# Layer 0: from TensorE transposes to a blocked second load, VectorE block transposes and a norm on ScalarE

## The chip, the cores and the metric

The kernel runs on one core of one Trainium2 chip. The time is device microseconds for one execution of the whole kernel (both layers). In the profile PE is TensorE (PEld its weight loads), DVE is VectorE, ACT is ScalarE, POOL is GpSimd, and SP is the engine whose queue issues nearly all DMAs.

## What is computed

`x` is 1 x 128 x 256 x 256 in float32. Two layers each add an attention branch to it. The first one, which the change touches, is this, cut to what matters here:

```python
def _gn(v, G=32, eps=1e-5):                 # mean and variance of 32 groups of 8 channels
    ...
    return ((g - m) / jnp.sqrt(s + eps)).reshape(v.shape)

def _L0_conv_ref(m, z, ...):                # m = _gn(x): 128 rows s, 256 positions i, 256 channels
    m_norm = layer_norm(m, ln_m_w, ln_m_b)  # over the channels
    q, k, v = m_norm @ Wq.T, m_norm @ Wk.T, m_norm @ Wv.T      # 8 heads of 32
    b = (z_norm @ Wb.T) ...                 # a bias for each head, the same for all rows s
    gate = jax.nn.sigmoid(m @ Wg.T + bg)
    scores = einsum('bsihc,bsjhc->bshij', q, k) * scale + b
    o = einsum('bshij,bsjhc->bsihc', softmax(scores), v)
    return (o * gate) @ Wo.T + bo

x = x + _L0_conv_ref(_gn(x), ...)
x = x + _L1_conv_ref(_gn(x), ...)           # banded attention, 4 heads of 64
```

## The kernel before, in words

**Stages.** A first stage (about 240 us) reads all of x for the group statistics and turns z into `eb`, the exponential of the bias. Layer 0 then works through 64 *pairs* of rows in about 1,830 us; layer 1 does its own 64 pairs in about 1,260 us. The change lies in layer 0, with a few operations added to the end of the first stage (`norm`).

**A pair.** A `Pair` loads two rows of x into `xt`, 128 partitions by 4 tiles of 256 channels, with positions on the partitions. `centre` and `scale` (POOL, L1233 and L1236) make `xg`, the group-normalised rows. `moments` (DVE) takes each position's mean and variance of `xg`; `root` (POOL) makes the inverse deviation `rs`. `send` stores it to DRAM and `fetch` reads it back spread over all partitions as `rs_r`. `turn` (L1274, L1278) is what the change replaces: TensorE transposes `xg` in eight 128x128 blocks into PSUM and ACT copies the result to `xgT`, channels on the partitions. `normal` (POOL, L1283) multiplies by `rs_r`, in two halves k = 0 and 1 of the channels, giving `xnT`. `project` (L1296, result moved from PSUM by ACT, L1300) makes qT and kT from `xnT` and the gate `gT` from `xgT`; `values` makes v from `xnT`. The layer norm's mean is folded into the weights.

**Attention.** `scores(r, c)` multiplies for row r and channel half c into two PSUM tiles (L1330), and ACT takes the exponential in place (L1337). `add_bias` multiplies by `eb` on DVE into two tiles `e` (L1346) and POOL adds the two key halves into `eboth` (L1351). `apply` makes the weighted values (`ps_ov`) and the sums (`ps_su`). `gate`, `invert` and `normalize` finish the division: `invert` takes the reciprocal, stores it to DRAM as `rsum`, and SP reads it back as four broadcasts `rvb`. `out_row` projects into PSUM and `keep_row` adds the residual.

**Order.** The order on every engine is the program's own (`manual_schedule`). One turn of the loop, 28.77 us long, interleaves five pairs: `old` and `was` are finishing, `now` is in its attention, `nxt` is being transposed and projected, `nn` is being normalised. In PE's order a turn is: scores(0,0), apply of `was`, projections qT and kT with m = 1, values(0), scores(0,1), the two gate projections, `old.out_row(1)`, scores(1,0), apply(0), `nxt.turn()`, values(1), scores(1,1), `nxt`'s projections qT and kT with m = 0, `was.out_row(0)`. All projections, values and output rows share a PSUM ring of two banks (`mm`, two buffers), so each of them needs the result of two steps earlier to have been moved out. The scores (and `ps_x` of `turn`) share the other ring, `ps_s`, of two buffers.

Of the kernel before, what the change touches and what calls it, by code (L numbers as in the profile page):

```python
# [9 lines left out]
F32 = mybir.dt.float32  # L10
AF = mybir.ActivationFunctionType
ALU = mybir.AluOpType
# [4 lines left out]
P = 128  # L17
# [4 lines left out]
def bcast(ap, axis, n):  # L22

    ap = ap.unsqueeze(axis)
    shape = list(ap.shape)
    shape[axis] = n
    return ap.broadcast_to(shape)
# [746 lines left out]
def fast_kernel(  # L774
# [25 lines left out]
    nc = tc.nc  # L800
    S, I, C = x.shape
    CZ = z.shape[2]
    H = wbT.shape[1]
    D0 = C // H
# [3 lines left out]
    NB = I // P  # L808
    KC = C // P
    NP = S // 2  # L810
    N2 = 2 * I
# [4 lines left out]
    const = ctx.enter_context(tc.tile_pool(name="const", bufs=1))  # L816
    dram = ctx.enter_context(tc.tile_pool(name="dram", bufs=1, space=DRAM))

    ident = const.tile([P, P], F32, name="ident")
# [111 lines left out]
    for a in range(KC):  # L931
        for h in range(H1):
            n = P // H1
# [5 lines left out]
    for h in range(H1):  # L939
        n = P // H1  # L940
# [57 lines left out]
    def mm(name):  # L998
        return ps_mm.tile([P, 512], F32, name=name, tag="mm")
# [199 lines left out]
    HQ = P // D0  # L1199
    NT = 2 * NB  # L1200
# [11 lines left out]
    for n in range(RC):  # L1212
# [2 lines left out]
            bcast(ident.rearrange("p (q d) -> p q d", q=HQ)[:, :, n * D0 // RC], 2, D0),  # L1215
        )

    class Pair:


# [7 lines left out]
            )  # L1228


        def centre(self):
            self.xg = la.tile([P, NT, C], F32, name="xg", tag="xg", bufs=2)
            nc.gpsimd.tensor_tensor(self.xg, self.xt, bcast(M0, 1, NT), ALU.subtract)  # L1233

        def scale(self):
# [226 lines left out]
    def some(n):  # L1462
        for _ in range(min(n, len(later))):
            later.pop(0)()
# [10 lines left out]
    def pair(p):  # L1475
        return Pair(p) if p < NP else Nobody()
# [20 lines left out]
    def norm():  # L1497
        nonlocal M0, R0, nxt
        M0, R0 = next(steps)
        now.centre()  # L1500
        now.scale()
        nxt = pair(1)

    def weigh():
# [5 lines left out]

    plan = {
        (0, 4): begin, (1, 1): lambda: next(steps), (1, 3): lambda: next(steps), (1, 4): take, (2, 3): norm,
        (3, 4): weigh,
        (5, 3): lambda: now.send(nc.scalar),
# [13 lines left out]
    behind, nx, n = None, 0, 0  # L1528
# [39 lines left out]
    su = ps_o.tile([P, I], F32, name="ps_su")  # L1568

    with tc.manual_schedule():  # L1570
        old = was = Nobody()
        es = nn3 = None
        for p in range(NP):

            nxt.root()
            nxt.send()
            e0 = now.add_bias(0, 0, now.scores(0, 0))
            was.apply(1, es)
            was.gate(1)
            was.invert()  # L1580
            nxt.fetch()
            nn.centre()
            if p == 0:
                nxt.residual()
            now.project("qT", 1)
            now.project("kT", 1)
            some(1 if p < NP - 2 else 3)
            now.values(0)
            now.keep_values(0)

            es = e0, now.add_bias(0, 1, now.scores(0, 1))
            nn.scale()
            if p == 0:
                now.residual()
            for m in range(KC):
                now.project("gT", m)
            old.out_row(1)
            some(1 if p < NP - 2 else 3)
            old.keep_row(1)

            nn3 = pair(p + 3)
            e0 = now.add_bias(1, 0, now.scores(1, 0))
            now.apply(0, es)
            now.gate(0)
            nxt.turn()
            nxt.normal()
            was.normalize(0)
            now.values(1)
            now.keep_values(1)
            nn.moments(0)  # L1610
            if p == NP - 1:
                some(8)

            es = e0, now.add_bias(1, 1, now.scores(1, 1))
            was.normalize(1)
            nn.residual()
            nxt.project("qT", 0)
            nxt.project("kT", 0)
            nn.moments(1)
            some(3 if p < NP - 2 else 9)  # L1620
            was.out_row(0)
            was.keep_row(0)
            old, was, now, nxt, nn = was, now, nxt, nn, nn3
        was.apply(1, es)
        was.gate(1)
        was.invert()
        old.out_row(1)
        was.spread()
        old.keep_row(1)
        for r in range(2):  # L1630
            was.normalize_last(r)
        for r in range(2):
            was.out_row(r)
            was.keep_row(r)
        some(len(later))
# [28 lines left out]
    with tc.tile_pool(name="l1", bufs=2) as sb, tc.tile_pool(  # L1664
        name="l1s", bufs=4
    ) as sm, tc.tile_pool(name="ps1_mm", bufs=2, space=PSUM) as ps_mm, tc.tile_pool(
        name="ps1_s", bufs=1, space=PSUM
    ) as ps_s, tc.tile_pool(name="ps1_o", bufs=1, space=PSUM) as ps_o:

        def mm1(name):  # L1670
            return ps_mm.tile([P, 512], F32, name=name, tag="mm")
# [173 lines left out]
        def pair1(p):  # L1845
            return Pair1(p) if p < NP else Nobody()
# [15 lines left out]
        with tc.manual_schedule():  # L1862
            now, nxt = pair1(0), pair1(1)
# [18 lines left out]
        with tc.manual_schedule():  # L1882
            was = Nobody()
            for p in range(NP - 1):
                nn = pair1(p + 2)
# [23 lines left out]
                was, now, nxt = now, nxt, nn  # L1909
# [19 lines left out]
        ps = mm1("ok_ps")  # L1929
# [4 lines left out]
@with_exitstack  # L1934
def mixer_kernel(ctx, tc, *args):

    nc = tc.nc
    keep = ctx.enter_context(tc.tile_pool(name="verdict", bufs=1))
    verdict = keep.tile([1, 1], mybir.dt.int32, name="verdict")
    fast_kernel(tc, *args, verdict)  # L1940
    again = nc.values_load(verdict[0:1, 0:1], min_val=0, max_val=1)
    with tc.If(again > 0):
        general_kernel(tc, *args)
# [53 lines left out]
```

## Time and profile before

| | |
|---|---|
| median of 3 runs | 3363.17 us (3362.63 to 3363.67) |
| span of the profiled execution, first to last instruction | 3356.3 us |
| so around the span | about 6.9 us |
| one turn of the layer 0 loop | 28.77 us |
| PE, busy share of the span | 96% |
| the 512 transposes of `turn` | 69.9 us busy, 273 ns each, overlapping |
| the 128 copies to `xgT` on ACT | 68.7 us busy, 589 ns each |
| POOL in a turn | 0.80 busy |
| DVE, ACT in a turn | 0.65 and 0.45 busy |
| DMA engines in a turn | about 0.23 busy |

The profile is one execution of the program. Busy times of different engines lie beside one another; PE's overlap even among themselves, since matmuls are pipelined. The row for the transposes is therefore not what they take out of PE's time; that is read from the starts of the groups in the timeline, or from the chain that ended last.

### The profile page before, as it was taken

How to read it: one execution, taken by the hardware profiler on the slowest of the kernel's cores; microseconds unless marked ns; L12 is line 12 of the kernel's file. 1: busy time of each engine (PE TensorE's matmuls, PEld its weight loads, DVE VectorE, ACT ScalarE, POOL GpSimd, SP SyncE). 2: the span in 40 equal slices, each digit the busy share in tenths (PEclk: the TensorE clock that was granted, in tenths of full speed). 3: DMA queues.
4: the chain of work that ended last, by engine and by line, in shares of the span. 5: the costliest groups of instructions: out<-in, count | busy, mean ns of one | idle time of the engine just before them, and what ended most of it. 6: DMA issues, size and time to landing. Idle time of an engine off the chain costs nothing.

```text
span 3356.3 us, 81416 instructions
## 1 busy us (share of the span) xinstructions
PE 3210.8 (96%) x35168; PEld 2039.6 (61%) x35168; DVE 2021.7 (60%) x3115; ACT 1461.1 (44%) x2121; POOL 1961.9 (58%) x1375
## 2 busy tenths in 40 slices
PE   5389999999999999999999998999999999999998
PEld 3255555555555555555555555667777677677676
DVE  7955666666666666666666666466544444443456
ACT  2264444444444444444444443344444444444443
POOL 2378787777777787887777774333333333333332
PEclk8699999999999999999999999999999999999999
DMA  9941212221222222122212221111211211112111
GB/s 350 369 135 43 74 49 74 74 74 49 74 74 57 58 71 68 49 74 74 74 49 74 74 65 47 64 53 53 65 53 53 65 53 58 60 53 61 57 58 53
DMA packets 198640, 262.39 MB, mean 78 GB/s; under 512 B 46240, under 2 KB 147488, under 8 KB 197120
## 3 DMA queue, kind: packets, MB, share of 16 engines
q1 hardware_dynamic: 193200, 254.19, 24.7%
q8 instruction: 279, 4.57, 0.6%
q10 hardware_dynamic: 5072, 2.90, 0.3%
q14 instruction: 89, 0.73, 0.1%
HBM read 188.30 MB, written 68.75 MB: 77 GB/s over the span
## 4 chain that ended last, share of the span: by engine, by line
PE 91%; DVE 4%; DMA 3%; ACT 1%; POOL 1%; issue 1%; SPq 0%; ACTq 0%; POOLq 0%; DVEq 0%
PE ps_p L1296 20%; PE ps_p L1743 14%; PE ps_sc L1330 8%; PE ps_y L1831 7%; PE ps_ov L1362 7%; PE ps_v L1758 7%; PE ps_y L1417 6%; PE ps_v L1311 6%; PE ps_o L1800 3%; PE ps_sc L1772 3%; PE ps_su L1370 3%; PE ps_x L1274 2%; PE ps_x L1730 2%; PE ps_su L1800 1%; DVE st L1178 1%; DVE zst L1103 1%
## 5 line engine op out<-in xcount | busy, mean ns | idle before, releaser
L1351 POOL TENSOR_TENSOR eboth<-e 128x512 f32<-128x512 f32 x512 | 639.9, 1271 | 391.7 <-DVE e L1346 389.7
L1346 DVE TENSOR_TENSOR e<-ps_sc,eb 128x1024 f32<-128x1024 f32 x512 | 603.2, 1220 | 304.9 <-ACT ps_sc L1337 304.8
L1337 ACT ACTIVATE ps_sc<-ps_sc 128x1024 f32<-128x1024 f32 x512 | 492.8, 1006 | 509.2 <-PE ps_sc L1330 509.2
L1782 POOL TENSOR_TENSOR e<-e,bw 128x384 f32<-128x384 f32 x256 | 258.7, 1031 | 444.3 <-ACT e L1780 444.3
L1743 PE MATMUL ps_p<-xgT,w_in 128*128 128x512 f32 x1024 | 469.2, 601 | 3.7 <-DVE w_in L1701 3.7
L1735 POOL TENSOR_TENSOR xt<-xt,bout_r 128x1024 f32<-128x1024 f32 x64 | 152.0, 2374 | 379.0 <-PE ps_x L1730 379.0
L1835 DVE TENSOR_TENSOR yo<-ps_y,xt 128x512 f32<-128x512 f32 x128 | 88.3, 690 | 379.1 <-PE ps_y L1831 379.1
L1743 PEld LDWEIGHTS ps_p<-xgT,w_in 128*128 128x128 f32 x1024 | 188.9, 190 | 203.0 <-issue 170.9
L1330 PE MATMUL ps_sc<-qT,kT 32*128 32x256 f32 x4096 | 293.3, 400 | 2.0 <-ACT kT L1300 2.0
L1296 PE MATMUL ps_p<-xnT,wq 128*128 128x512 f32 x512 | 266.0, 631 | 3.5 <-POOL xnT L1283 2.9
L1831 PE MATMUL ps_y<-w_out,oT 128*128 128x256 f32 x1024 | 249.1, 386 | 2.6 <-DVE oT L1816 2.6
L1362 PE MATMUL ps_ov<-e,v 128*32 128x256 f32 x4096 | 247.7, 382 | 0.0
L1417 PEld LDWEIGHTS ps_y<-wo,oT 128*128 128x128 f32 x1024 | 194.3, 190 | 82.4 <-issue 59.3
L1417 PE MATMUL ps_y<-wo,oT 128*128 128x256 f32 x1024 | 242.0, 379 | 2.0 <-POOL oT L1407 1.2
L1330 PEld LDWEIGHTS ps_sc<-qT,kT 32*128 32x128 f32 x4096 | 184.9, 184 | 94.4 <-issue 83.6
L1311 PE MATMUL ps_v<-wv,xnT 128*128 128x256 f32 x1024 | 242.2, 379 | 0.0
L1296 PE MATMUL ps_p<-xnT,wk 128*128 128x512 f32 x512 | 240.6, 592 | 0.0
L1296 PE MATMUL ps_p<-xgT,wg 128*128 128x512 f32 x512 | 236.8, 605 | 0.0
L1758 PE MATMUL ps_v<-w_in,xgT 128*128 128x256 f32 x1024 | 231.8, 379 | 0.0
L1813 DVE RECIPROCAL rv<-odd 128x256 f32<-128x256 f32 x128 | 224.4, 1753 | 4.4
L1758 PEld LDWEIGHTS ps_v<-w_in,xgT 128*128 128x128 f32 x1024 | 194.4, 190 | 53.5 <-issue 30.1
L1311 PEld LDWEIGHTS ps_v<-wv,xnT 128*128 128x128 f32 x1024 | 189.6, 190 | 50.8 <-issue 31.0
(170 smaller groups left out, 4958.8 us busy)
## 6 DMA issues: line engine op xcount, KB each, us to landing
xa<-in_x_dram SPq DMA_DIRECT2D x8, 4096.0 KB
xt<-in_x_dram SPq DMA_DIRECT2D x64, 512.0 KB
x<-xo SPq DMA_DIRECT2D x16, 2048.0 KB
xt<-x SPq DMA_DIRECT2D x64, 512.0 KB
rvb<-rsum SPq DMA_DIRECT2D x252, 128.0 KB
out_dram<-yo SPq DMA_DIRECT2D x63, 512.0 KB
zt<-in_z_dram SPq DMA_DIRECT2D x15, 2048.0 KB
rs_r<-rs_d SPq DMA_DIRECT2D x63, 256.0 KB
```

The costliest lines, as they stand in the source:

```text
L1296: nc.tensor.matmul(ps, w[:, k, m * P : (m + 1) * P], getattr(self, src)[:, k, :], start=(k == 0), stop=(k == KC - 1),)
L1311: nc.tensor.matmul(self.ps_v[:, b * C : (b + 1) * C], self.xnT[:, k, t * P : (t + 1) * P], wv[:, k, :], start=(k == 0), stop=(k == KC - 1),)
L1330: nc.tensor.matmul(self.pss[q // 2][:, q % 2, b, :], self.kT[rs, c, r * I + b * P : r * I + (b + 1) * P], self.qT[rs, c, r * I : (r + 1) * I],
L1337: nc.scalar.activation(self.pss[a], self.pss[a], AF.Exp)
L1346: nc.vector.tensor_tensor(e, pss[a], eb[:, h : h + 2], ALU.mult)
L1351: nc.gpsimd.tensor_tensor(t, es[a][:, :, 0, :], es[a][:, :, 1, :], ALU.add)
L1362: nc.tensor.matmul(ov[q * D0 : (q + 1) * D0, c, :], self.v[:, r, b, h * D0 : (h + 1) * D0], es[q // 2][:, q % 2, b, :], start=(b == 0), st ...
L1417: nc.tensor.matmul(self.ps_y[:, b * C : (b + 1) * C], self.oT[r][:, k, b * P : (b + 1) * P], wo[:, k, :], start=(k == 0), stop=(k == KC - 1),)
L1743: nc.tensor.matmul(ps, w_in[:, k, n * C + m * P : n * C + (m + 1) * P], self.xgT[:, k, :], start=(k == 0), stop=(k == KC - 1),)
L1758: nc.tensor.matmul(ps[:, b * C : (b + 1) * C], self.xgT[:, k, t * P : (t + 1) * P], w_in[:, k, 2 * C : 3 * C], start=(k == 0), stop=(k == ...
L1782: nc.gpsimd.tensor_tensor(e[:, q], e[:, q], bcast(bw.rearrange("p b w -> p (b w)"), 1, KC), ALU.mult)
L1831: nc.tensor.matmul(ps[:, b * C : (b + 1) * C], self.oT[r][:, k, b * P : (b + 1) * P], w_out[:, k, :], start=(k == 0), stop=(k == KC - 1),)
```

## The change

For all pairs but the first, `turn` leaves the loop. `blocks` loads the pair's two rows a second time into `xs`, by four DMAs on SP's queue, one for each j of 4. Partition j*32+b then holds, for each n, channel half k and row block, the run of 32 channels `(k, j)` of the position that belongs to b: runs of 128 bytes, 1,024 in each DMA. `turn_blocks` transposes the 32x32 blocks on DVE, two instructions of 128x512, into `xgT`. This is raw x, so `scale_blocks` normalises it on ACT, in place, with two activations that take scale and bias from a column per channel half (`col`). The columns are made once, in `norm`, by four small matmuls and two DVE operations. In the loop `nxt.turn_blocks()` and `nn.blocks()` stand after `now.keep_values(0)`, and `nxt.scale_blocks()` after `nn.scale()`, ahead of the gate projections. `xg` goes from two buffers to one. POOL's `centre` and `scale` stay, because the moments still need `xg`.

```diff
+    col = const.tile([P, 2, KC], F32, name="col")
...
+        def blocks(self):
+
+            self.xs = la.tile([P, NB, KC, 2 * HQ, D0], F32, name="xs", tag="xs", bufs=1)
+            by_block = x[2 * self.p : 2 * self.p + 2].rearrange(
+                "s (i b n) (k j a) -> j b (n k) (s i) a", i=HQ, n=NB, k=KC, a=D0
+            )
+            for j in range(HQ):
+                nc.sync.dma_start(self.xs[j * D0 : (j + 1) * D0].rearrange("b n k i a -> b (n k) i a"), by_block[j])
+
+        def turn_blocks(self):
+            self.xgT = la.tile([P, KC, N2], F32, name="xgT", tag="xgT", bufs=2)
+            for n in range(NB):
+                nc.vector.transpose(
+                    self.xgT.rearrange("p k (s n i b) -> p n k s i b", s=2, n=NB, i=HQ)[:, n],
+                    self.xs[:, n].rearrange("p k (s i) a -> p k s i a", s=2),
+                )
+
+        def scale_blocks(self):
+            for k in range(KC):
+                nc.scalar.activation(
+                    self.xgT[:, k, :], self.xgT[:, k, :], AF.Identity,
+                    bias=col[:, 1, k : k + 1], scale=col[:, 0, k : k + 1],
+                )
+
         def centre(self):
-            self.xg = la.tile([P, NT, C], F32, name="xg", tag="xg", bufs=2)
+            self.xg = la.tile([P, NT, C], F32, name="xg", tag="xg", bufs=1)
...
         M0, R0 = next(steps)
+        ps = mm("ps_col")
+        for n, row in enumerate((R0, M0)):
+            for k in range(KC):
+                nc.tensor.matmul(
+                    ps[:, n * KC + k : n * KC + k + 1], row[:, k * P : (k + 1) * P], ident[:, 0:1],
+                    start=True, stop=True,
+                )
+        nc.vector.tensor_copy(col[:, 0], ps[:, 0:KC])
+        nc.vector.scalar_tensor_tensor(col[:, 1], ps[:, KC : 2 * KC], -1.0, col[:, 0], ALU.mult, ALU.mult)
         now.centre()
...
     with tc.manual_schedule():
+        nxt.blocks()
         old = was = Nobody()
...
             now.values(0)
             now.keep_values(0)
+            nxt.turn_blocks()
+            nn.blocks()
 
             es = e0, now.add_bias(0, 1, now.scores(0, 1))
             nn.scale()
+            nxt.scale_blocks()
             if p == 0:
                 now.residual()
             for m in range(KC):
...
             now.gate(0)
-            nxt.turn()
             nxt.normal()
```

## The prediction

> **What bounds the kernel now.** I read the page's busy shares first, then the chain that ended last, then one turn of layer 0 on each engine. The page and the chain:
>
> ```profile
> PE 3210.8 (96%) x35168; PEld 2039.6 (61%) x35168; DVE 2021.7 (60%) x3115; ACT 1461.1 (44%) x2121; POOL 1961.9 (58%) x1375
> PE 91%; DVE 4%; DMA 3%; ACT 1%; POOL 1%; issue 1%; SPq 0%; ACTq 0%; POOLq 0%; DVEq 0%
> ```
>
> So PE sets the time on average, and work taken from PE looks like time gained. Whether it is depends on what is late next at that place. Pieces of the chain in one turn, start and length:
>
> ```profile
> 999.89 1.86 PE ps_ov L1362 x32
> 1001.76 0.86 PE ps_su L1370 x16
> 1002.62 1.02 PE ps_x L1274 x8
> 1003.64 1.73 PE ps_v L1311 x8
> 1005.37 1.08 PE ps_sc L1330 x16
> 1006.45 3.81 PE ps_p L1296 x8
> ...
> 1015.79 3.63 PE ps_p L1296 x8
> ```
>
> The eight transposes take 1.02 us of PE. The next ps_x starts at 1031.39, so a turn is 28.77 us. The same projection takes 3.63 us elsewhere and 3.81 here: PE already waits 0.18 us inside it. The timelines of PEld and POOL say for what:
>
> ```profile
> 1007.42 0.30 PEld L1296 LDWEIGHTS ps_p<-xnT,wq 128*128 128x128 f32 x2 [0.74 <-POOL xnT L1283]
> ...
> 1002.41 2.51 POOL L1351 TENSOR_TENSOR eboth<-e 128x512 f32<-128x512 f32 x2 [1.63 <-DVE e L1346]
> 1004.86 2.50 POOL L1283 TENSOR_TENSOR xnT<-xgT,rs_r 128x512 f32<-128x512 f32 x2
> ```
>
> The second half of xnT ends at 1007.36, PE continues at 1007.42. Before xnT, POOL does eboth of scores(1,0), having idled 1.63 us for e. This chain hangs on scores(1,0) ending on PE (999.89): exp, e, two eboth, two xnT, 7.5 us. It runs beside exactly the PE steps among which the transposes stand.
>
> The second place is ACT, DVE and SP around scores(0,1):
>
> ```profile
> 1022.26 1.93 ACT L1337 ACTIVATE ps_sc<-ps_sc 128x1024 f32<-128x1024 f32 x2 [2.11 <-PE ps_sc L1330]
> 1024.18 0.69 ACT L1300 ACTIVATE gT<-ps_p,bg_c 128x512 f32<-128x512 f32 x1
> ...
> 1021.19 0.69 DVE L1317 TENSOR_TENSOR v<-ps_v,vb_r 128x512 f32<-128x512 f32 x1 [2.14 <-PE ps_v L1311]
> 1023.37 2.36 DVE L1346 TENSOR_TENSOR e<-ps_sc,eb 128x1024 f32<-128x1024 f32 x2 [1.49 <-ACT ps_sc L1337]
> ...
> 1025.69 1.89 PE L1417 MATMUL ps_y<-wo,oT 128*128 128x256 f32 x8
> ...
> 1027.17 0.37 SPq L1264 DMA_DIRECT2D rs_r<-rs_d  x1
> ```
>
> The first gT leaves PSUM from 1024.18 to 1024.87. The ring has two banks, so out_row(1), at 1025.69, needs that bank. It has 0.8 us to spare today.
>
> **What the skill says.** Four pages are used; only prices follow from them. "TensorE: Matmul & The Clock Gate", Part 4, gives about 275 ns for a transpose in a kernel; the trace agrees (273 ns), but as they overlap the cost is 1.02 us for eight. "VectorE: DVE Perf Modes", The three transpose paths, says that DVE only turns 32x32 blocks, 311 ns for 128x128 of 2-byte data; the trace has none. "ScalarE: Activation LUTs", What ACT_TABLE_LOAD costs, gives 280 + 0.833 N ns with a per-partition bias, 93 ns more for a per-partition scale, and 93 ns of overlap between neighbours; for N = 512 that is 707, and L1300 measures 687. "DMA: Bandwidth & Descriptors", the section on why a DMA adds 16 to its semaphore, says that a descriptor moves one contiguous run: here 128 bytes.
>
> **Part by part.**
>
> *Transposes removed.* 63 turns by 1.02 us = 64 us less PE work; their ACT copies (1.07 us for two) ended in idle time and bring nothing. What is late next: without them PE reaches the projection at 999.89 + 1.86 + 0.86 + 1.73 + 1.08 = 1005.42. xnT does not come earlier. `normal` keeps its place behind eboth, POOL works without a gap from 1002.41, and eboth waits for e, not for xgT. PE thus waits 1.02 + 0.18 = 1.20 us instead of 0.18, and goes on at 1007.42 as before. **Gain: 0.** Scores(1,1) comes a microsecond earlier; eboth(1,1) is queued behind xnT and a normalize, so that moves nothing.
>
> *Two ACT activations added* between the second exp and the first gT. From SBUF with scale and bias columns an estimate is 707 + 93 = 0.80 us each, 0.71 apart. Bounds: 0.59 (the plain copy L1278) and 0.87. The exps end at 1024.19; with 0.09 us of overlap the two start at 1024.10 and 1024.81, gT starts at 1025.52 instead of 1024.18 and ends at 1026.21. PE can write that bank at 1026.27, not 1025.69: 0.58 us late; bounds 0.14 and 0.72, and up to 0.12 more if the wait also holds back the weight load. I take 0.6. Behind it on PE stands scores(1,0), from which the 7.5 us chain hangs, and nothing in the turn has slack to return. 62 turns (the first has no `old`) by 0.6 = **37 us longer**; bounds 9 and 52.
>
> *Two DVE transposes added*, 512 elements for each partition. At one element a cycle they resemble a 128x512 tensor_tensor (0.69 us, 0.60 apart): from 1021.8 to 1023.1, inside the 1.49 us in which DVE idles before e. **Cost 0.** Lower bound the same. Upper: half rate, an estimate of (2 x 0.53 + 0.16) = 1.2 us each, end at 1024.2: the ACT step starts 0.1 late, and e(0,1) ends at 1026.6, still ahead of scores(1,0) at 1027.51. Without that cover every further microsecond delays scale_blocks, then gT, then out_row(1); e(0,1) and the scores behind it follow.
>
> *Four DMAs added each turn* on SP, 4,096 runs. SP issues are about 0.4 us each (rvb, L1391), so SP is held some 1.7 us. They stand behind fetch (1027.17), when turn_blocks (1023.1) is long done, so SP does not wait for xs to be free. Behind them: the load of pair p+3 (three turns early), x1 stores, and the next send (1044.7). Transfer: with 16 engines 256 runs each. The trace has no such load. From below, the 512 four-byte writes of send, which took 0.11 + 0.14 us of engine share, 8 ns a run; from above, 47 ns for 1 KB runs (16 engines moving 350 GB/s in the first slice). So 2 to 12 us of engine time; send's 512 runs spread over 2 us suggest up to 4 ns of queue time a run, 16 us. I take 12: landed by about 1041, needed at 1050.6. They queue behind rvb and rs_r and are through before the next rsum store at 1047.6. DMA's 0.23 share rises. **Cost 0**; no gain is possible here.
>
> *xg with one buffer.* centre comes at 1018.35; the last reader, moments, is done at 1010.5. Cost 0. *The col operations, once:* PE takes four small matmuls (0.35 us each by the similar b_ps row), DVE waits for them; the next DVE work there idles 3.3 us for z data. 0 to 3 us, I take 1.5. *The first blocks* queue behind the last z load on the same queue, 40 us ahead of use: 0.
>
> **Sum.** Against the profiled execution: 3356.3 + 6.9 around the span = 3363.2, just the median; + 0 + 37 + 1.5 = **3402 us**.
>
> **Rivals.**
>
> 1. *The cover works (no change, 10%).* ACT needs as little as the copies (0.54 apart) and the wait on PSUM is 0.15 us or less: 0 to 9 us more, 3363 to 3372; in favour is only that no SBUF activation of this form is in the trace.
> 2. *Faster (8%).* PE's wait for xnT isn't the end of a full POOL queue: if xnT were ready 1 us earlier, so that PE at 1005.42 finds it, each turn gains up to 1.02 - 0.6 = 0.4 us, 62 x 0.4 = 26 us: 3338. It decides from the point where xnT's second half ends before 1006.3. For it: POOL's times are called rough, and the xgT copies end at 1004.81, near xnT's start. Against it: POOL shows no idle there, and PE restarts 0.06 us after xnT's end.
> 3. *Block data or turns come late (12%).* If a run costs over 80 ns an engine (20 us a turn), rsum and rs_r queue behind it; at 100 ns the DMA engines need 25.6 + 6.6 = 32 us a turn, 3.4 over: 3363 + 63 x 3.4 = 3580. If DVE's transposes took 2.3 us each, gT would be 2.8 us late: 3363 + 62 x 2.8 = 3537. For it: runs of 128 bytes, unseen so far. Against it: the 8 and 47 ns.
> 4. That the loop still transposes on PE is excluded: only pair 0 calls turn.
>
> **How the numbers follow.** The main case has 70%. About 0.2% (7 us) is what a measurement of this kernel can tell from no change. The main case alone gives 3372 to 3418. Rival 1 spreads over the 0.2% line, nearly all of it on the side of no change. The range 3366 to 3425 takes in the main case with its bounds, part of rival 1, and the mild form of rival 3; outside lie rival 2 and the heavy forms of 3. Faster 0.08, same 0.10, slower 0.82.
>
> **What would show it.** Right: PE's wait for xnT L1283 grows to about 1.2 us a turn; ps_x has 8 matmuls; a new wait of PE or PEld at L1417 for ACT gT, near 0.6 us a turn; the turn takes 29.4 us; DVE's idle before e(0,1) shrinks to near 0.2 us. Wrong: a turn under 28.77 us, a PE wait at scores(1,0) for e, or DVE idle for a DMA of xs.

## The result, and the profile after

The changed kernel takes 3410.19 us (median; 3407.36 to 3411.1), the kernel before 3362.9 us; the ratio is 1.014, with a 95% interval of 1.0125 to 1.0154. Slower, as predicted (3402, range 3366 to 3425). In the profiled executions the span grew by 49.3 us, from 3356.3 to 3405.6.

First the page: busy shares, then the shares of the chain that ended last.

```profile
PE 3185.4 (94%) x34672; PEld 1983.7 (58%) x34672; DVE 2129.6 (63%) x3243; ACT 1470.2 (43%) x2121; POOL 1958.9 (58%) x1375
PE 66%; DVE 9%; POOL 7%; ACT 6%; issue 5%; DMA 5%; SPq 1%; POOLq 0%; ACTq 0%; DVEq 0%
```

PE is listed as busy for 25 us less. That is less than the 64 us of the transposes, above all because a wait inside a group of matmuls counts as busy (the first projection below is listed with 2.36 us, one without a wait in the same turn with 1.98). And yet the end comes later: the chain spends 66% on PE where it spent 91%, and the rest now runs through DVE, POOL and ACT. A chain that changes engines like this is a chain of waits. Which ones, the timeline of PE over one turn shows (start, length, and in brackets the idle time before it and who ended that):

```profile
1000.51 2.36 PE L1322 MATMUL ps_p<-xnT,wq 128*128 128x512 f32 x4 [0.56 <-POOL xnT L1309]
...
1016.48 3.70 PE L1322 MATMUL ps_p<-xgT,wg 128*128 128x512 f32 x8
1020.65 1.97 PE L1443 MATMUL ps_y<-wo,oT 128*128 128x256 f32 x8 [0.47 <-ACT gT L1326]
...
1023.62 1.93 PE L1388 MATMUL ps_ov<-e,v 128*32 128x256 f32 x32
...
1026.35 1.99 PE L1337 MATMUL ps_v<-wv,xnT 128*128 128x256 f32 x8
1028.27 1.15 PE L1356 MATMUL ps_sc<-qT,kT 32*128 32x256 f32 x16
1029.98 2.36 PE L1322 MATMUL ps_p<-xnT,wq 128*128 128x512 f32 x4 [0.56 <-POOL xnT L1309]
```

From one xnT projection to the next: 1029.98 - 1000.51 = 29.47 us, where a turn took 28.77. Two waits are in it. One is for POOL's xnT, where the transposes had stood; it grew, but adds nothing, as shown below. The other is new: out_row(1) waits for ACT's gT. The views of PE's waits and of the weight loads (PEld) add them up for all turns (us in total, times, longest), and show the loads of this step:

```profile
PE ps_p L1322 <- POOL xnT L1309: 39.3, 63, 3.5
PE ps_y L1443 <- ACT gT L1326: 28.0, 60, 0.5
```

```profile
1020.62 1.59 PEld L1443 LDWEIGHTS ps_y<-wo,oT 128*128 128x128 f32 x8 [1.27 <-POOL eboth L1377]
...
1031.21 0.30 PEld L1322 LDWEIGHTS ps_p<-xnT,wq 128*128 128x128 f32 x2 [0.94 <-POOL xnT L1309]
```

All eight weight loads of out_row(1) stand behind the wait. In the kernel before, the first was issued ahead, beside the last gate matmul, and seven followed:

```profile
1025.27 0.19 PEld L1417 LDWEIGHTS ps_y<-wo,oT 128*128 128x128 f32 x1 [0.24 <-issue]
1025.69 1.49 PEld L1417 LDWEIGHTS ps_y<-wo,oT 128*128 128x128 f32 x7 [0.24 <-issue]
```

(The eboth named in the first of these views is no input of out_row; the PE row names the right releaser, gT, which is moved out of the PSUM bank that out_row needs.) Why gT is late, ACT's timeline shows:

```profile
1016.59 1.92 ACT L1363 ACTIVATE ps_sc<-ps_sc 128x1024 f32<-128x1024 f32 x2 [2.11 <-PE ps_sc L1356]
1018.41 1.52 ACT L1252 ACTIVATE xgT<-xgT,col 128x512 f32<-128x512 f32 x2
1019.82 1.26 ACT L1326 ACTIVATE gT<-ps_p,bg_c 128x512 f32<-128x512 f32 x2
```

Exp, scale, gT, without a gap. The two scales take 1.52 us, and both gates wait until they are through. The first gT, 0.69 long, ends near 1020.5, and PE writes the bank at 1020.65. Measured from the first gate matmul, out_row(1) now comes 1020.65 - 1016.48 = 4.17 us later; it was 1025.69 - 1022.16 = 3.53. That is 0.64 more. These are the gates, out_row(1) and the scores behind it in the kernel before:

```profile
1022.16 3.70 PE L1296 MATMUL ps_p<-xgT,wg 128*128 128x512 f32 x8
1025.69 1.89 PE L1417 MATMUL ps_y<-wo,oT 128*128 128x256 f32 x8
1027.51 1.15 PE L1330 MATMUL ps_sc<-qT,kT 32*128 32x256 f32 x16
```

Out_row's own step is 1.90 us (1020.65 to the next scores, 1022.55) instead of 1.82, since no weight load is ahead: 0.08 more. Together 0.72, against the 0.70 by which the turn grew.

DVE's and SP's timelines show the parts predicted to cost nothing:

```profile
1015.52 0.69 DVE L1343 TENSOR_TENSOR v<-ps_v,vb_r 128x512 f32<-128x512 f32 x1 [2.15 <-PE ps_v L1337]
1016.12 1.29 DVE L1245 STREAM_TRANSPOSE xgT<-xs 128x512 f32<-128x512 f32 x2
1017.70 2.36 DVE L1372 TENSOR_TENSOR e<-ps_sc,eb 128x1024 f32<-128x1024 f32 x2 [0.28 <-ACT ps_sc L1363]
```

```profile
1020.35 0.37 SPq L1290 DMA_DIRECT2D rs_r<-rs_d  x1
1020.81 4.42 SPq L1240 DMA_DIRECT2D xs<-in_x_dram  x4
1025.33 1.27 SPq L1227 DMA_DIRECT2D xt<-in_x_dram  x1
```

The transposes lie in DVE's idle time and leave 0.28 us of it. The four loads hold SP for 4.42 us and are not waited for in the turn.

**Where the 49.3 us are.** I cut the span at two marks that every kernel here has: the first scores of the loop, and the last apply (`ps_ov`) of layer 0.

| | before | after | difference |
|---|---|---|---|
| start of the loop (first scores) | 238.75 | 244.43 | +5.7 |
| loop, first scores to last apply | 1834.8 | 1877.6 | +42.8 |
| from there to the end | 1282.8 | 1283.6 | +0.8 |

Of the 42.8, the first turn has 1.2 (26.40 to 27.56). The other 41.6 fall on the 61 turns that have both an `old` and a pair to scale: 0.68 each, near the 0.70 of the turn shown. The 1.2 of the first turn are a matter of PE's clock. PE waits for xnT there in both kernels, and the projection behind that wait takes 2.35 us before and 3.52 after:

```profile
260.30 2.35 PE L1296 MATMUL ps_p<-xnT,wq 128*128 128x512 f32 x4 [2.71 <-POOL xnT L1283]
```

```profile
265.97 3.52 PE L1322 MATMUL ps_p<-xnT,wq 128*128 128x512 f32 x4 [3.53 <-POOL xnT L1309]
```

In the windows of the traces the granted clock of PE, as a share of full speed, is 1.00 from 260.3 to 262.5 before, and 0.50 from 266 to 269 after. That the longer wait made it fall is not shown: in the experiment below with the col operations alone, which keeps the transposes, the clock is 0.50 behind a wait of 2.72 us as well (268.1 to 271.5).

### The profile page after: what moved, and what is told of

The parts are those of the page before. It is cut to its first block, busy times and chain, and to the rows that moved or that the text cites. A ratio compares the mean times of both kernels' runs of the same rounds, so it can differ in the third digit from the quotient of the medians.

```text
span 3405.6 us, 80748 instructions
## 1 busy us (share of the span) xinstructions
PE 3185.4 (94%) x34672; PEld 1983.7 (58%) x34672; DVE 2129.6 (63%) x3243; ACT 1470.2 (43%) x2121; POOL 1958.9 (58%) x1375
## 4 chain that ended last, share of the span: by engine, by line
PE 66%; DVE 9%; POOL 7%; ACT 6%; issue 5%; DMA 5%; SPq 1%; POOLq 0%; ACTq 0%; DVEq 0%
PE ps_p L1781 13%; PE ps_p L1322 11%; PE ps_y L1869 7%; PE ps_v L1796 7%; PE ps_y L1443 6%; POOL xnT L1309 4%; PE ps_sc L1356 4%; PE ps_o L1838 3%; ACT ps_sc L1363 3%; PE ps_ov L1388 3%; PE ps_sc L1810 3%; PE ps_v L1337 3%; DVE e L1372 3%; POOL eboth L1377 2%; DVE xgT L1245 2%
```

## The experiments

### The scales behind the gates

The new kernel with one line moved: ACT scales xgT after it has moved both gates out of PSUM.

```diff
             nn.scale()
-            nxt.scale_blocks()
...
             for m in range(KC):
                 now.project("gT", m)
+            nxt.scale_blocks()
```

> The changed kernel with scale_blocks moved behind the two gate projections, nothing else. Theory A (removing the transposes gains nothing because xnT's chain over POOL fills the gap; the 0.70 us a turn come from the two activations ahead of gT): the wait of out_row(1) for gT goes, the turn is again 28.77 us (within 0.05), PE still waits about 1.2 us a turn for xnT; time about 3410 - 61 x 0.70 = 3367 us. Theory B (the transposes' 1.02 us are a real gain, hidden only by the wait for gT): turn about 27.75 us, time about 3305 us. Theory C (the extra DMAs and DVE transposes slow the turn): turn stays at 29.4 us, time about 3410 us.

Measured: 3367.65 us, ratio 1.0022 (1.0014 to 1.0029). The timeline of PE:

```profile
1003.43 3.70 PE L1322 MATMUL ps_p<-xgT,wg 128*128 128x512 f32 x8
1006.96 1.89 PE L1443 MATMUL ps_y<-wo,oT 128*128 128x256 f32 x8
...
1016.21 2.35 PE L1322 MATMUL ps_p<-xnT,wq 128*128 128x512 f32 x4 [0.56 <-POOL xnT L1309]
...
1032.17 2.41 PE L1322 MATMUL ps_p<-xgT,wg 128*128 128x512 f32 x5
```

Out_row(1) follows 3.53 us after the gates again, without a wait. The turn is 1032.17 - 1003.43 = 28.74 us, the loop 1836.3, which is 1.5 above the kernel before; the first turn alone is 2.5 longer (28.87 instead of 26.40), with a granted clock of 0.50 from 268 to 273. So the place of two activations on ACT is the whole loss in the turns. The DMAs, the DVE transposes and the single buffer of xg are all still in this kernel: in the turns they cost nothing that can be seen. And the wait for xnT is untouched, so 8 fewer transposes a turn bring nothing.

### The transposes removed, and nothing put in their place

The kernel before, without `turn`: ACT copies xg to xgT as it lies, which no matmul has to prepare. There is no load of xs, no DVE transpose, no scale, no col. (xgT then has the wrong arrangement.)

```diff
-            nxt.turn()
+            nxt.stand_in()      # two nc.scalar.copy from xg to xgT
             nxt.normal()
```

> The kernel before without the eight TensorE transposes in the loop: xgT is copied by ACT straight from xg, untransposed, so xgT holds the wrong arrangement; no DMA, DVE or scaling step is added. It measures what the removal alone is worth. Theory A: nothing; turn 28.77 us, PE waits about 1.2 us a turn for xnT instead of 0.18, time 3363 us within 4. Theory B: 63 x 1.02 = 64 us faster, 3299 us, turn 27.75 us.

Measured: 3359.86 us, ratio 0.9998 (0.9989 to 1.0007). Its PE timeline:

```profile
1002.83 1.93 PE L1367 MATMUL ps_ov<-e,v 128*32 128x256 f32 x32
...
1005.56 1.99 PE L1316 MATMUL ps_v<-wv,xnT 128*128 128x256 f32 x8
...
1009.19 2.35 PE L1301 MATMUL ps_p<-xnT,wq 128*128 128x512 f32 x4 [0.56 <-POOL xnT L1288]
...
1031.59 1.93 PE L1367 MATMUL ps_ov<-e,v 128*32 128x256 f32 x32
```

A turn of 28.76 us. 64 us of transposes taken from an engine that is 96% busy, and the time is the same: here the cover of the chain scores(1,0), exp, e, eboth, xnT is seen by itself. It also shows where the 1.02 us went. The first and second half of the projection wait for xnT: 1009.19 comes 1.70 us after the scores ahead of it instead of 1.08, and kT (1011.38) 2.19 after qT instead of 1.82, together 1.0 us, of which the kernel before had 0.18. The other 0.2 went into values(1): it follows the sums directly and takes 1.93 us to the next step (1005.56 to 1007.49); in the chain of the kernel before, where it follows the transposes, it took 1.73.

### The chain for xnT moved forward as well

If xnT is what PE waits for, bringing it forward must release the gain. The kernel with the scales behind the gates, and `normal` ahead of scores(1,0) and the POOL work that hangs on it; the fetch of rs_r goes ahead of `invert` on SP, so that it is there in time.

```diff
+            nxt.fetch()
             was.invert()
-            nxt.fetch()
             nn.centre()
...
+            nxt.normal()
             e0 = now.add_bias(1, 0, now.scores(1, 0))
             now.apply(0, es)
             now.gate(0)
-            nxt.normal()
             was.normalize(0)
```

> scale_late, and in addition fetch (rs_r) issued ahead of invert, and normal (xnT on POOL) placed ahead of add_bias(1,0), so that xnT no longer stands behind eboth of scores(1,0). Theory A: PE's wait for xnT vanishes, 1.20 us a turn; turn about 27.57 us, time about 3367 - 62 x 1.2 = 3293 us, up to 3310 if another wait appears. Theory B: as scale_late, nothing more to gain.

Measured: 3300.76 us, ratio 0.9823 (0.9807 to 0.984), faster than both kernels. From the timelines of POOL and PE:

```profile
1012.27 2.53 POOL L1309 TENSOR_TENSOR xnT<-xgT,rs_r 128x512 f32<-128x512 f32 x2
```

```profile
1014.07 1.99 PE L1337 MATMUL ps_v<-wv,xnT 128*128 128x256 f32 x8
1016.00 1.15 PE L1356 MATMUL ps_sc<-qT,kT 32*128 32x256 f32 x16
1017.07 1.98 PE L1322 MATMUL ps_p<-xnT,wq 128*128 128x512 f32 x4
```

xnT is done at 1014.8, PE needs it at 1017.07, and no step of PE in the turn waits. The turn is 1032.67 - 1004.91 = 27.76 us, the loop 1769.0. I had expected 27.57 = 28.77 - 1.02 - 0.18. The 0.19 between is values(1) again, 1014.07 to 1016.00. With the transposes gone, the PE time that can be won is 1.02 - 0.19 = 0.83 us a turn, not 1.02.

### The same reordering with the transposes kept

The kernel before in that order, with `turn` behind the gate projections: what does the order alone bring?

```diff
+            nxt.fetch()
             was.invert()
-            nxt.fetch()
...
                 now.project("gT", m)
+            nxt.turn()
...
+            nxt.normal()
             e0 = now.add_bias(1, 0, now.scores(1, 0))
...
-            nxt.turn()
-            nxt.normal()
```

> The kernel before, with TensorE's transposes kept, but turn placed right behind the gate projections, fetch issued ahead of invert and normal ahead of add_bias(1,0), as in normal_early. It tells how much of normal_early's gain is the freed PE time and how much the new order. Theory A (the two add: 0.18 us a turn of waiting, then 1.02 us of transposes): turn 28.77 - 0.18 = 28.59 us, time about 11 us under the kernel before, ratio 0.9966. Rival: the new order alone gives most of the gain, turn near 27.6 us, ratio near 0.98.

Measured: 3351.23 us, ratio 0.9951 (0.9936 to 0.9966). Here the turn is 28.63 us (apply(0) at 999.17 and at 1027.80). Against 27.76 the transposes are worth 0.87 us a turn, close to the 0.83 above. So the order alone brings 0.14 of the 1.01 us a turn, or 10.7 of the 65.8 us of the loop (1834.8 us before, 1824.1 here, 1769.0 with both); the larger part belongs to the freed PE time. By the ratios (0.9951 for the order alone, 0.9823 for both) the order's share is larger; there is no trace of the kernel before from this chip that would place the difference. The idea of the change had been worth that all along, once the next chain was out of the way.

### The fetch left at its old place

The reordered kernel, with the fetch behind `invert` as before, in a single execution.

```diff
-            nxt.fetch()
             was.invert()
+            nxt.fetch()
```

> normal_early with fetch left at its old place behind invert's broadcasts. Normal, now ahead of eboth of scores(1,0) on POOL, must wait for rs_r, issued about 15.2 us after scores(0,0) starts. Theory A: rs_r lands about 4.5 us after its issue, xnT is done about as late as PE needs it; turn between 27.6 and 28.3 us, with POOL waiting for the DMA of rs_r 1 to 2 us a turn. Rival: the early fetch is immaterial, no such wait on POOL, turn 27.57 us.

Measured: 3457.55 us, slower than every other kernel here, and a miss. POOL's timeline:

```profile
1024.02 2.49 POOL L1309 TENSOR_TENSOR xnT<-xgT,rs_r 128x512 f32<-128x512 f32 x2 [5.08 <-DMA rs_r<-rs_d]
1026.47 2.50 POOL L1377 TENSOR_TENSOR eboth<-e 128x512 f32<-128x512 f32 x2
```

xnT, now early in POOL's queue, waits 5.08 us for rs_r (265.3 us in 61 turns), and with it the eboth and normalize queued behind. I had placed the fetch by its order and worked out its landing as if the rest of the turn stood still. But it is issued 17.6 us after scores(0,0) on average, not 15.2: on SP it stands behind the broadcasts of rsum, and these wait longer for the store of rsum to land than in the changed kernel. The waits of SP's queue, first here, then in the changed kernel:

```profile
SPq L1417 <- DMA rsum<-rv: 459.3, 63, 9.7
```

```profile
SPq L1417 <- DMA rsum<-rv: 331.3, 63, 7.0
```

Why that store takes longer is not shown. The turns take 28.4 to 35.0 us, 30.2 on average; the one of the timeline takes 30.86 (apply of `was` at 1002.38 and 1033.24).

### The start of the loop: the col operations alone

The kernel before with only the four small matmuls and two DVE operations in `norm`, in a single execution.

```diff
         M0, R0 = next(steps)
+        ps = mm("ps_col")        # four matmuls, then two DVE operations to col
```

> The kernel before with only the small matmuls and DVE operations that make col added in norm (col is not used). It tells what of the 5.7 us later start of the loop (first scores(0,0) at 244.43 us instead of 238.75) comes from PE waiting for R0 in the z stage. Theory P (that wait holds up z's transposes and with them the release of z buffers): start 2 to 4 us later, about 241 to 242.5. Theory Q (the early xs loads between the z loads are the cause): start at 239 us, unchanged within 0.5. Turn 28.77 us in both.

Measured: 3368.18 us; the loop starts at 246.53. The timelines of DVE and of ACT in the first stage:

```profile
180.84 0.16 DVE L1509 COPY col<-ps_col 128x2 f32<-128x2 f32 x1 [1.96 <-PE ps_col L1505]
```

```profile
181.85 0.59 ACT L1127 COPY zT<-ps_t 128x512 f32<-128x512 f32 x1 [5.58 <-PE ps_t L1125]
```

In the program's order on PE the transposes of z stand behind these matmuls, and the matmuls wait for R0. ACT's copies of z idle 5.58 us for them, the z buffer comes free later, and the next z load is issued at 188.57, where the kernel before has 181.85. That is more than the 2 to 4 us expected, and the clock has a part in it. The transposes of z behind these matmuls take 3.65 us here, and 2.02 in the changed kernel, which has the same matmuls ahead of them:

```profile
180.67 3.65 PE L1125 MATMUL ps_t<-ident,zt 128*128 128x128 f32 x16
```

```profile
178.94 2.02 PE L1125 MATMUL ps_t<-ident,zt 128*128 128x128 f32 x16
```

The granted clock is 0.50 from 180.7 to 184.2 here, and 1.00 in the changed kernel from 176 to 190.

### The new kernel with the col operations later

The new kernel with these operations in the next step, `weigh`, behind the moments, in a single execution.

> The changed kernel with the col operations moved from norm to weigh, where R0 has long been there; the early xs loads stay. Theory P (PE's wait for R0 is the cause of the later start): first scores(0,0) about 5.5 us earlier than in scale_late's 246.35, near 241 us, and the time about 3405 us. Theory Q (the xs loads between the z loads): start stays near 246 us. Turn 29.47 us in both.

Measured: 3406.44 us; start of the loop 243.66, turn 29.47 as in the changed kernel. Later than without either edit (below), so the first block loads take a share too.

### A best version, three attempts

First the reordered kernel, with the col operations in `weigh` and the first block loads behind the first `send` instead of ahead of the loop:

> normal_early with the col operations in weigh and the first xs loads issued behind the first send in the loop. Theory A: turn 27.57 us as in normal_early, start of the loop 5 us earlier; time about 3296 us, ratio to the kernel before about 0.981. Rival: the start is bound by the z loads of that run and not by col, then it equals normal_early, 3301 us.

Measured: 3313.91 us, ratio 0.9839 (0.9826 to 0.9853), no better than the reordered kernel alone. The start is at 241.40, as hoped, but then DVE's timeline says

```profile
257.41 1.31 DVE L1245 STREAM_TRANSPOSE xgT<-xs 128x512 f32<-128x512 f32 x2 [8.78 <-DMA xs<-in_x_dram]
```

The first loads issue in 10.4 us and land too late: the first turn takes 33.1 us, where the reordered kernel has 24.0, and the gain of the start is lost in it. Later turns lose as much again: the loop is 1787.0 us instead of 1769.0, and xnT waits for rs_r for 67.1 us in all, where it waited for 7.0. So the loads stay ahead of the loop; next, only the col operations moved, beside the reordered kernel once more on the same chip:

> The reordered loop of normal_early, with one edit more: the col operations leave norm for weigh, after the moments and root. The first block loads stay ahead of the loop. Theory P (the start of the loop is late mostly because PE waits for R0 in the middle of the z stage, which the col operations put there; the first block loads between the last z loads cost some 2 us): the loop's first scores start at about 244, where normal_early has 250, the first turn doesn't wait for xs as it did in best, and the whole takes 4 to 6 us less than normal_early, 3296 to 3300 at the clock of its run, ratio to the kernel before 0.980 to 0.982. Theory Q (the col operations cost nothing on their own and the block loads take the time wherever they stand, as best suggested): start near 249, ratio 0.983 to 0.984.

> The reordered loop alone, once more, on the same chip as best2 for the comparison of the two: ratio 0.982 to 0.984, start of the loop near 249, turn 27.76.

Measured: 3328.69 us, 0.9841 (0.9827 to 0.9854), and 3328.72 us, 0.9844 (0.9831 to 0.9857). The start came 2.7 us sooner (243.42 and 246.11), the end did not. This chip needs 3383.34 us for the kernel before, and the reordered kernel has turns over 28.5 us on it, 28.2 on average. Why the kernel before is slower here is not known, since there is no trace of it from this chip. For the reordered kernel the waits of POOL and of SP's queue point to a cause:

```profile
POOL xnT L1309 <- DMA rs_r<-rs_d: 118.9, 57, 4.5
```

```profile
SPq L1290 <- DMA rs_d<-lrs: 598.1, 63, 12.0
```

The store of the inverse deviations takes 9.5 us on average until the fetch can follow it; in the first run of this kernel it took 8.2 (519.0 in 63), and xnT waited for rs_r 7.0 us in all. The reordered kernel stands at the edge of this chain. On POOL its `root` stands behind a `residual` that nobody needs yet, so the last pair of kernels moves that into an idle stretch behind `centre`; the second of them also has the col operations in `weigh`.

```diff
             nn.centre()
-            if p == 0:
-                nxt.residual()
+            nxt.residual()
...
-            nn.residual()
```

> normal_early with POOL's residual (the addition of bo_r to xt, 2.4 us) moved from ahead of root to behind centre, where POOL idles 3.1 us for e. In normal_early_again the inverse deviation waits from 1000.8 (DVE's lrs) to 1005.5 (POOL's root) behind a normalize and this residual; then the store takes 10.6 us, the load 4.7, and xnT waits 2.1 us a turn for rs_r, in 57 turns. Theory E (this chain now sets part of the turn): root and rs_r come 2.4 us sooner, xnT's wait for rs_r falls under 0.3 us a turn, PE's waits for oT at out_row (13.2 us) go, turns of 27.8 us throughout: about 20 us under normal_early on such a chip, ratio 0.978 to 0.981. Theory F (those waits lie beside PE's own work, and PE at 27.75 us a turn is the bound anyhow): ratio 0.984 as before.

> resid_later with the col operations in weigh as well. The 2.7 us that best2 gained at the start of the loop (243.42, where normal_early_again had 246.11) were lost again in turns that waited for rs_r. If theory E holds, they stay: 2 to 4 us less than resid_later, ratio 0.977 to 0.980. If the start is lost in the first turns anyhow: the same as resid_later.

Measured: 3299.78 us, 0.9822 (0.9808 to 0.9835), and **3296.94 us, 0.9813 (0.9799 to 0.9826)**, the fastest kernel of the study. The timeline of PE in the latter:

```profile
1003.64 1.93 PE L1388 MATMUL ps_ov<-e,v 128*32 128x256 f32 x32
...
1031.40 1.93 PE L1388 MATMUL ps_ov<-e,v 128*32 128x256 f32 x32
```

27.76 us a turn, a loop of 1768.0 us, and hardly any wait for xnT. Both are above what theory E expected. What the residual's move is worth stays open: this chip runs the kernel before in 3360.07 us and stores rs in 8.3 us, so most of the wait that the move was to end may not have been there, and the two orders were never on one chip. The 2.8 us between the two come with the move of the col operations, the only edit between them; 1.7 of them are seen at the start of the loop (243.12 instead of 244.78).

### All starts of the loop

| col in `norm` | first xs loads ahead of the loop | first scores, us |
|---|---|---|
| no | no | 238.75 (before), 240.93 (nothing in the transposes' place), 241.79 (order alone), 241.40 (first attempt at a best version) |
| yes | no | 246.53 |
| no | yes | 243.66, 243.42, 243.12 |
| yes | yes | 244.43 (after), 244.78, 246.11, 246.35, 250.08, 250.46 |

The loads alone make some 2.7 us (mean 243.4 against 240.7). For the col operations it is 5.8 in the one run, 3.6 by the means of the last two rows. But the last row spreads over 6 us, and the granted clock goes with that spread. Where it stays at 1.00 behind PE's wait for R0 (2.63 us), the loop starts at 244.43 and 244.78. Where it falls to 0.50 behind that wait, for 3 to 6 us, it starts at 246.11 and 246.35; where it does so and is down to 0.50 again from 243 to 246, at 250.08 and 250.46. With the full clock the col operations thus cost some 1.2 us. Why the clock falls in one execution and not in another is not shown.

## Why the prediction was right, and where its sizes were off

- **Transposes removed, gain 0: shown**, twice over: removal alone leaves the time the same, and the scales moved out of the way give back the turn of before and nothing more. Of the predicted wait of 1.20 us instead of 0.18, about 1.0 came; 0.2 went into values(1), which I had left at 1.73. What stands ahead of a matmul group also changes that group's step: in the timeline of the kernel before, values(1) takes 1.82 us behind the transposes, and 1.92 in the last turn, which has none (2067.95 to 2069.87).
- **ACT's activations, 0.6 us a turn: the mechanism shown, the size 0.70.** From the Trainium skill's page "ScalarE: Activation LUTs", What ACT_TABLE_LOAD costs, I took estimates of 0.80 us each and 0.71 apart; measured are 812 ns and 1.52 us for the two. The 0.58 I had worked out for the delay was 0.64, and the weight load that the wait holds back, which I left as "up to 0.12", was 0.08. I counted 62 turns, and 61 have both sides of it. The term is 41.6 us where I took 37.
- **DVE transposes, cost 0: right.** One takes 686 ns, predicted 690, the time of a tensor_tensor of that size. The Trainium skill's page "VectorE: DVE Perf Modes", The three transpose paths, prices only 2-byte data. DVE's remaining idle time, 0.28 us, is near the 0.2 that I named.
- **DMAs, cost 0 in the turn: right, the size off both ways.** They hold SP 4.42 us in the turn shown, not 1.7: I took the issue time of other DMAs for them. The data was through sooner than the 12 us. In the windows of the trace the DMA engines are busy 0.97 from 1021 to 1025, 0.82 to 1029, and 0.03 after that: at most 8.2 us from the first issue. Over the 32 us that I compared it is 9.4 us of busy engines instead of 5.2, 4.2 more, or 16 ns for each of an engine's 256 runs, between the 8 and 47 that I had as bounds.
- **xg with one buffer, cost 0: right**, as it is still so in the kernels that lose nothing in their turns.
- **The start of the loop: the wrong term.** I took 1.5 us for the col operations and 0 for the first blocks; the profiled starts lie 5.7 apart. About 2.0 of that is spread: the kernel before has the earliest start of the four in the first row of the table (238.75, mean 240.7). The blocks account for 2.7, and 1.0 is left for col in this execution, where the clock stayed full. So the 0 for the blocks was the miss. They did not "queue behind the last z load": SP's timeline has their first issues at 160.91 and 185.69, among the z loads. For col the size held here, but the reasoning did not: I asked what DVE waits for, not what is queued behind PE's wait for R0, which is the z transposes, and through their buffers the z loads. Alone, and with the clock at 0.50, it cost 5.8. The 1.2 us of the first turn (the clock) and the 0.8 behind the loop were in no step; the cause of the 0.8 was not tried.

Against the profiled spans I predicted 38.5 us more and got 49.3. The 10.8 are 4.2 at the start, 5.8 in the loop and 0.8 behind it, all on the same side, so the hit does not rest on errors that cancel. Of the rivals, the second (faster) asked for xnT a microsecond earlier: that was not so in this kernel, and where it was made so, with the scales moved as well, the gain came.

## What to carry to other kernels

Work taken off the busiest engine is a gain only as far as nothing else is due at the same place: ask which chain the engine would meet next. A wait of 0.18 us at the next step was enough to say that a microsecond of saved work would be worth none, and a kernel that only leaves the work out tests it for the price of one run. An operation moved to a half-idle engine costs its length, less the slack at that place, where it stands ahead of a result that frees a buffer (1.52 us of activations cost 0.72 here), and nothing a few steps later; and before a chain is brought forward, follow it through every queue that it passes, since the next chain in line here (rs through two DMAs) was late at once when it met one wait more, and on one chip by itself.

## What was not expected of the hardware

- Loads in runs of 128 bytes: 512 KB in 4,096 runs, with its neighbours, was through in at most 8.2 us in the middle of the kernel. Issuing is dearer than the data suggests: four of them hold the queue for 4.42 us in the turn shown, and 10.4 at the start of the loop in the first attempt at a best version.
- A wait for a PSUM bank also takes away the weight load that would have run ahead: 0.08 us on a group of eight.
- The same values(1) takes 1.73 us behind transposes and 1.92 behind the small matmuls of the sums (in the chains of the kernel before and of the reordered one). The reason was not tried.
- A store of 512 four-byte elements takes 8.2 to 9.5 us until the load that follows it can be issued, not the same from chip to chip. The waits of the reordered loop for rs_r go with it: 7.0 us in all at 8.2, 67.1 at 9.0 (the first attempt at a best version), 118.9 at 9.5. That the store is their cause was not tried by itself.
- The granted clock can fall behind a short wait of PE: to 0.50, for 3 us or more, behind 3.53 us in the first turn of the changed kernel and behind 2.64 us in the first stage of the kernel with the scales behind the gates, but it stayed at 1.00 behind 2.63 us in the first stage of the changed kernel and behind 2.71 in the first turn of the kernel before.
